# A graph layer and a mixture of experts on one core: side pieces placed two to four chunks further behind their operands

## The chip, the core and the metric

The kernel runs on one core of a Trainium2 chip. The core has a matrix engine (TensorE, "PE" in the profile, with its weight loads as "PEld"), a vector engine (VectorE, "DVE"), a scalar engine (ScalarE, "ACT"), a general engine (GpSimd, "POOL") that here mostly issues indirect DMAs, and SyncE ("SP"), whose queue issues all plain DMAs. Each engine works through its own list of instructions in order and waits on semaphores for the others. The metric is the device time of one execution in microseconds (us).

## The reference

There are N = 6250 nodes with D = 256 features, 106250 edges sorted by destination, and 8 experts with H = 1024 hidden units.

```python
# graph layer
xw  = layernorm(x) @ W
msg = xw[src] * rsqrt(max(out_deg, 1))[src][:, None]
agg = segment_sum(msg, dst)
x   = x + relu(agg * rsqrt(max(in_deg, 1))[:, None] + b)
# mixture of experts, two experts a token
xt = layernorm(x); logits = xt @ Wr + br
top_p, top_idx = top_k(softmax(logits), 2); weights = top_p / top_p.sum()
xe = layernorm(xt) * ln_g[e] + ln_b[e]          # for each expert e
y  = gelu(xe @ W1[e] + b1[e]) @ W2[e] + b2[e]
x  = x + sum over the two experts of weight * y
```

## The kernel before, in words

**Head.** The out-degrees are counted with one-hot matmuls, and a table of scaled rows `ytab` is written to device memory.

**The gather loop.** The edges are cut into 831 chunks of 128 edges; 14 chunks (`CE`) make a block, and there are 60 blocks. The loop over `CHUNKS` at the end of the kernel writes the order of the instructions out by hand: for chunk `i` it emits, in this order,

- an indirect DMA on POOL for chunk `i + LEAD` (`LEAD = 24`; `gather`, L1271), and at most one waiting scatter of routed rows (`send`, L965, into `xs`) or scatter-add of results (`add_up`, L1095, into `out`);
- the chunk's own matmuls on PE, which add its 128 rows into the block's sum `pm` by a one-hot of the destinations (L1372 up to chunk 168, after that three bf16 matmuls, L1375 to L1377, from rows of a second table `ptab`). The rows lie in a ring of 28 buffers, so the gather for chunk `c + 28` waits until PE is done with chunk `c`;
- every seven chunks the next one-hots on DVE (L223);
- side pieces, up to a budget (`run_side`, 1.2);
- pieces of the experts' work (`run_steps`), at a rate that the planner sets.

**Side pieces** are Python generators. `yield cost, wait` ends a piece and says how many chunks later the next piece may stand. They are:

- `finish(b)`, when block `b` is summed: ACT copies `pm` to `ag` (L735); a later piece turns it on PE (L741, L742) and DVE adds the result into a ring of sums (L747).
- `tile_sums(t)`, when all edges of node tile `t` are in: PE multiplies with the graph layer's weights (L781, L785), DVE computes the degree's root, the relu, and adds `x` (tile `x2`, L796), SP stores it to `out` (L807).
- `route_group(g)`, for a group of two to four tiles (`GS`): the second layernorm on DVE (L838), transposes on PE (L860), their copy on ACT (L862), logits on PE (L849), softmax and the choice of two experts on DVE and ACT, counts by matmul (L922, L923), positions on DVE, then the scatter of the rows and a list of expert steps (`batches`).

**Expert steps** (`expert_steps`). One step takes 256 rows of one expert (128 in the first eight): SP loads the rows (`xin`, L1131) and the expert's 2182 KB of weights (`w`, L1136); PE transposes (L1144), DVE scales (L1149), PE runs the first layer (L1201, into `ph`, two buffers), ACT the gelu (L1210), PE the second layer (L1220), DVE the output (L1231, L1237), POOL adds it to `out`. The planner turns a batch of steps into a rate: estimated cost of what is waiting over the chunks left until the next batch is expected (`expect`), at most 1.3 a chunk.

**Tail.** After the last chunk the remaining steps follow each other; the last batch holds ten, and more under a condition.

The tiles `x2` of the nodes' features are loaded two blocks ahead (`fetch_x`, L767) and held until the group is routed. The ring of sums is made of segments of 1024 nodes; `later` holds when the next segment's start values are loaded (`open_segment`).

Of the kernel before, what the change touches and what calls it, by code (L numbers as in the profile page):

```python
# [9 lines left out]
F32 = mybir.dt.float32  # L10
# [8 lines left out]
P = 128  # L19
# [4 lines left out]
def gnn_then_moe(  # L24
# [51 lines left out]
    NMSG = 42  # L76
    LEAD = 24
    BEHIND = 10

    TB = 256  # L80
    SB = TB // P
# [626 lines left out]
    side = []  # L708
    batches = []

    def register(engine, ap, top):
        _, (v,) = nc.values_load_multi_w_load_instructions(
            ap, engines=(engine,), min_val=0, max_val=top,
            skip_runtime_bounds_check_because="made from counts that stay in range",
            bass_reorder=False,
        )
        return v
# [13 lines left out]
    def finish(b, pm):  # L731

        s = seg(b)
        ag = s3.tile([P, D + 1], F32, tag="ag", name="ag")
        nc.scalar.copy(ag, pm)  # L735
        if b and seg(b - 1) < s:
            nc.vector.tensor_copy(ring[s][:, :, :OVER], ring[s - 1][:, :, SEGN:])
        yield 0.0, 2
        pt = psum()[:, : (KD + 1) * P].rearrange("p (k q) -> p k q", q=P)
        for k in range(KD):  # L740
            nc.tensor.transpose(pt[:, k, :], ag[:, k * P : (k + 1) * P], ident)  # L741
        nc.tensor.matmul(  # L742
            pt[:, KD, :], ag[:, D : D + 1].to_broadcast([P, P]), ident,
            start=True, stop=True,
        )
        w = register(mybir.EngineType.DVE, win_i[0:1, b : b + 1], RING - WIN)
        nc.vector.tensor_tensor(  # L747
            ring[s][:, :, bass.ds(w, WIN)], ring[s][:, :, bass.ds(w, WIN)], pt, ALU.add
        )
        for t in range(NT):  # L750
            if CLOSE[t] == b:
                side.append([now[0] + 2, 1, tile_sums(t, ring[s], t * P - SEGN * s)])
        yield 0.7, 1

    place = {}
# [6 lines left out]
    x_of = {}  # L762

    def fetch_x(t):
        v = x_of[t] = s3.tile([P, D], F32, tag="x2", name="x2", bufs=17)
        if t < NT - 1:
            nc.sync.dma_start(v, x[t * P : (t + 1) * P, :])  # L767
        else:
            nc.vector.memset(v, 0.0)
            for r0, r1 in ((0, split), (split, LASTROWS)):  # L770
                nc.sync.dma_start(v[r0:r1, :], x[t * P + r0 : t * P + r1, :])

    def tile_sums(t, sums, c0):

        g, i = place[t]
        if i == 0:
            held[g] = s3.tile([P, GMAX, 2], F32, tag="mv1", name="mv1")
        x2, mv1 = x_of[t], held[g]
        pw = psum()
        for k in range(KD):  # L780
            nc.tensor.matmul(  # L781
                pw[:, :D], sums[:, k, c0 : c0 + P], gw_sb[:, k, :],
                start=(k == 0), stop=(k == KD - 1),
            )
        nc.tensor.matmul(  # L785
            pw[:, D : D + 1], sums[0:1, KD, c0 : c0 + P], ones[0:1, 0:1],
            start=True, stop=True,
        )
        deg = s3.tile([P, 1], F32, tag="deg", name="deg")
        nc.vector.tensor_scalar(deg, pw[:, D : D + 1], 1.0, None, op0=ALU.max)  # L790
        nd = rsqrt(s3, deg, 1, "nd")
        h = s3.tile([P, D], F32, tag="h", name="h")
        nc.vector.scalar_tensor_tensor(
            h, pw[:, :D], nd, gb_sb, op0=ALU.mult, op1=ALU.add
        )
        nc.vector.scalar_tensor_tensor(  # L796
            x2, h, 0.0, x2, op0=ALU.max, op1=ALU.add
        )
        st = s3.tile([P, 6], F32, tag="bnst", name="bnst")
        nc.vector.bn_stats(st, x2)  # L800
        nc.vector.bn_aggr(mv1[:, i, :], st)
        if t < NT - 1:
            parts = ((0, P),)
        else:
            parts = ((0, split), (split, LASTROWS))
        for r0, r1 in parts:
            d = nc.sync.dma_start(out[t * P + r0 : t * P + r1, :], x2[r0:r1, :])  # L807
            for o in adds:
                tc.declare_no_dep(d.ins, o.ins, reason="rows of other tokens")
            bases.append(d)  # L810
        yield 1.1, 1
        if i == GS[g] - 1:
            side.append([now[0] + 3, 2, route_group(g, t + 1 - GS[g], mv1)])

    def running(bufs, first, n):
        a, d, i = first, 1, 0
# [7 lines left out]
    def route_group(g, t0, mv1):  # L824
# [11 lines left out]
        for q in range(n + 2):  # L836
# [15 lines left out]
                    )  # L852
                nc.vector.tensor_tensor(logits[:, i, :], pl, br_sb, ALU.add)
            if q == 0:
                yield 0.0, 2
            if 0 <= q - 1 < n:
                i = q - 1
                pt = psum()[:, : KD * P].rearrange("p (k q) -> p k q", q=P)
# [1 line left out]
                    nc.tensor.transpose(pt[:, k, :], rowt[:, i, k * P : (k + 1) * P], ident)  # L860
                turned[i] = s3.tile([P, KD, P], F32, tag="xtT", name="xtT", bufs=3)
                nc.scalar.copy(turned[i], pt)  # L862
            yield 0.9, 1
        rs2 = rsqrt(s3, mv2[:, :n, 1], n, f"l2_{n}", EPS)
        shift = s3.tile([P, GMAX], F32, tag="shift", name="shift")[:, :n]
        nc.vector.scalar_tensor_tensor(
# [31 lines left out]
        for s in range(2):  # L898
# [16 lines left out]
            if has_last:  # L915
                j = s * n + n - 1
                nc.vector.tensor_scalar(hot[:, j, :], hot[:, j, :], valid, None, op0=ALU.mult)
        yield 0.0, 4
        hotf = hot.rearrange("p j e -> p (j e)")
        w2 = 2 * n * E  # L920
        pp = psum()
# [201 lines left out]
    def expert_steps(todo, forever):  # L1123
# [133 lines left out]
    closing = {b: [t for t in range(NT) if CLOSE[t] == b] for b in range(NBE)}  # L1257

    expect = [
        end_of[CLOSE[sum(GS[: g + 1]) - 1]] + 3 * GS[g] + LEAD + 16 for g in range(len(GS))  # L1260
    ]
    def gather(i):
        b, j = CHUNKS[i]
# [81 lines left out]
    for i, (b, j) in enumerate(CHUNKS):  # L1345
# [41 lines left out]
        if i + 1 == end_of[b]:  # L1387
            side.append([i + 1, 0, finish(b, pm)])
            if b + 1 < NBE and seg(b + 1) > seg(b) and seg(b + 1) + 1 < NSEG:
                later.append((i + CE, seg(b + 1) + 1))  # L1390
        if later and later[0][0] <= i:
            open_segment(later.pop(0)[1])
        run_side(1.2)
# [101 lines left out]
```

## Time and profile before

| | |
|---|---|
| Median of 10 runs | 1903.2 us (1898.85 to 1912.02) |
| The profiled execution | 1899.83 us, of which the span of instructions is 1898.1 us |
| PE busy over the span | 1439.7 us (76%) |
| PE weight loads | 1171.0 us (62%) |
| DVE busy | 875.7 us (46%) |
| ACT busy | 395.0 us (21%) |
| POOL busy | 1153.1 us (61%) |
| Mean granted clock of TensorE | 0.877 |
| First and last chunk's matmul | 147 us and 1619 us |
| Time after the last chunk in which PE runs expert steps alone | from 1671 us on

How to read the views used below. A row of a *table by stretches* gives for each engine the busy time in that stretch, the granted TensorE clock (1.00 is full speed) and the share of time in which the DMA engines were busy. A row of *waits* says which engine sat idle before which instruction, what ended the wait, the total, how often, and the longest; `issue` and `remote` mean that the profile names nobody. A row of *groups* reads: line, engine, operation, tiles, how many | busy us, mean ns | idle time before, and what ended it. A row of a *timeline* gives start, duration, engine, line, operation, tiles, how many, and in brackets the idle time before it. Matmuls are pipelined and their ends are modelled.

### The profile page before, as it was taken

The numbers are of one execution on the slowest core, as the hardware profiler recorded it, in microseconds if no ns is written. First come the engines' busy times: TensorE is split into PE (matmuls) and PEld (weight loads), VectorE is DVE, ScalarE is ACT, GpSimd is POOL, SyncE is SP. The second block draws the span as 40 slices with busy tenths as digits, with TensorE's granted clock in tenths as the row PEclk, the third lists the DMA queues.
The fourth block names the chain that finished last, engine by engine and source line by source line (L and its number), as shares of the span: only waits on it lengthen the run. The fifth ranks groups of instructions, "written<-read, shape, count | busy, mean of one in ns | idle before, by whom it ended". The sixth has DMA issues, their size and how long they took to land. (4 is left out here: it accounts for less than half of the span.)

```text
span 1898.1 us, 23690 instructions
## 1 busy us (share of the span) xinstructions
PE 1439.7 (76%) x7890; PEld 1171.0 (62%) x7890; DVE 875.7 (46%) x3123; ACT 395.0 (21%) x978; POOL 1153.1 (61%) x1127
## 2 busy tenths in 40 slices
PE   6966454547576898767777778797789799799997
PEld 5854343446355676546556566576577587688886
DVE  8993364435253372534524435326256354732211
ACT  3662121002020121210211112112112212322221
POOL 8837767466766666667666666765766563423322
PEclk9997677778777898979789889898899799899998
DMA  7737665277575776657566676576677576576673
GB/s 223 269 115 250 192 196 186 83 275 231 175 240 182 269 230 231 192 182 232 179 217 211 197 253 193 186 240 214 198 241 231 175 232 208 152 250 189 199 218 74
DMA packets 146583, 389.50 MB, mean 205 GB/s; under 512 B 22316, under 2 KB 89364, under 8 KB 139282
## 3 DMA queue, kind: packets, MB, share of 16 engines
q0 software_dynamic: 70176, 179.11, 34.1%
q1 hardware_dynamic: 76218, 208.73, 30.4%
q8 instruction: 66, 1.08, 0.2%
q14 instruction: 67, 0.55, 0.1%
q10 hardware_dynamic: 56, 0.02, 0.0%
HBM read 324.26 MB, written 63.52 MB: 204 GB/s over the span
## 5 line engine op out<-in xcount | busy, mean ns | idle before, releaser
L1271 POOL DMA_INDIRECT msgs<-ptab,srcT x663 | 653.9, 986 | 339.3 <-issue 131.8
L1201 PE MATMUL ph<-xeT,w 128*128 128x256 f32 (+1 forms) x1792 | 457.2, 393 | 79.3 <-issue 54.7
L1220 PE MATMUL py<-w,hT 128*128 128x256 f32 x1664 | 432.8, 395 | 19.6 <-issue 16.4
L1201 PEld LDWEIGHTS ph<-xeT,w 128*128 128x128 f32 x1792 | 334.4, 208 | 127.2 <-issue 61.3
L1210 ACT ACTIVATE hT<-ph,w 128x256 f32<-128x256 f32 (+1 forms) x448 | 180.6, 456 | 853.1 <-PE ph L1201 359.8
L1220 PEld LDWEIGHTS py<-w,hT 128*128 128x128 f32 x1664 | 305.9, 198 | 55.9 <-issue 17.9
L1095 POOL DMA_INDIRECT out_x<-yo,to_all x86 | 137.9, 1604 | 179.8 <-DVE yo L1237 34.7
L1375 PE MATMUL pm<-msgs,oh 128*128 128x257 bf16 x663 | 191.3, 289 | 6.4 <-issue 6.3
L1376 PE MATMUL pm<-msgs,oh 128*128 128x256 bf16 x663 | 190.3, 287 | 6.8 <-issue 6.8
L1377 PE MATMUL pm<-msgs,oh 128*128 128x256 bf16 x663 | 190.1, 287 | 6.0 <-issue 6.0
L1149 DVE TENSOR_SCALAR xeT<-ptf,w 128x256 f32<-128x256 f32 (+1 forms) x112 | 53.5, 519 | 258.6 <-PE ptf L1144 128.6
L747 DVE TENSOR_TENSOR ring<-ring,misc 128x384 f32 x60 | 33.3, 554 | 287.0 <-remote 163.4
L1271 POOL DMA_INDIRECT msgs<-ytab,srcT x126 | 128.8, 1022 | 54.9 <-issue 33.3
L965 POOL DMA_INDIRECT xs<-rowt,pos_i x98 | 100.1, 1021 | 58.3 <-issue 44.7
L223 DVE TENSOR_TENSOR oh<-iota_w,relT 128x896 bf16<-128x896 f32 (+2 forms) x119 | 127.7, 1080 | 14.5 <-PE pm L1372 8.2
L781 PE MATMUL misc<-gw_sb,ring 128*128 128x256 f32 x196 | 70.9, 497 | 78.6 <-issue 40.5
L1372 PE MATMUL pm<-msgs,oh 128*128 128x257 f32 x336 | 103.0, 461 | 29.6 <-DVE oh L223 14.8
L1376 PEld LDWEIGHTS <-oh 128*128 128x128 bf16 x663 | 68.4, 103 | 76.2 <-issue 20.4
L1372 PEld LDWEIGHTS pm<-msgs,oh 128*128 128x128 f32 x336 | 74.4, 233 | 43.3 <-DVE oh L223 15.6
L781 PEld LDWEIGHTS misc<-gw_sb,ring 128*128 128x128 f32 x196 | 43.3, 243 | 93.5 <-issue 45.6
L381 PE MATMUL hist<-oh_hi,oh_lo 128*128 128x49 bf16 x831 | 85.4, 279 | 11.4 <-DVE oh_lo L375 10.9
L381 PEld LDWEIGHTS <-oh_lo 128*128 128x128 bf16 x831 | 82.5, 150 | 14.2 <-DVE oh_lo L375 13.8
(600 smaller groups left out, 1591.7 us busy)
## 6 DMA issues: line engine op xcount, KB each, us to landing
w<-in_wcat SPq DMA_DIRECT2D x56, 2182.0 KB
xin<-xs SPq DMA_DIRECT2D x48, 260.0 KB
msgs<-ptab,srcT POOLq DMA_INDIRECT x663
strayT<-zeros SPq DMA_DIRECT2D x1, 9216.0 KB
ptab<-part SPq DMA_DIRECT2D x24, 384.0 KB
ytab<-xres SPq DMA_DIRECT2D x7, 896.0 KB
ring<-strayT SPq DMA_DIRECT2D x4, 1536.0 KB
x<-in_x SPq DMA_DIRECT2D x48, 128.0 KB
```

Of the source, the lines that this page charges most:

```text
L223: nc.vector.tensor_tensor(oh[:, :n, :], iota_w[:, None, :].to_broadcast([P, n, WIN]), relT[:, c : c + n, None].to_broadcast([P, n, WIN]), ...
L381: nc.tensor.matmul(hist, oh_lo[:, :, c], oh_hi[:, :, c], start=(c0 + c == 0), stop=(c0 + c == NCH - 1),)
L781: nc.tensor.matmul(pw[:, :D], sums[:, k, c0 : c0 + P], gw_sb[:, k, :], start=(k == 0), stop=(k == KD - 1),)
L1095: ad = nc.gpsimd.indirect_dma_start(out=out, out_offset=bass.IndirectOffsetOnAxis(ap=to, axis=0), in_=rows, in_offset=None, compute_op=ALU ...
L1201: nc.tensor.matmul(ph[:, c - c0, :tb], w[:, k * H + c * P : k * H + (c + 1) * P], xeT[:, k, :tb], start=(k == 0), stop=(k == KD - 1),)
L1210: nc.scalar.activation(hT[:, c, :tb], ph[:, c - c0, :tb], AF.Gelu, bias=w[:, OB1 + c : OB1 + c + 1],)
L1220: nc.tensor.matmul(py[:, s, :], hT[:, c, s * P : (s + 1) * P], w[:, OW2 + c * D : OW2 + (c + 1) * D], start=(c == 0), stop=(c == HC - 1),)
L1271: nc.gpsimd.indirect_dma_start(out=to, out_offset=None, in_=table, in_offset=bass.IndirectOffsetOnAxis(ap=srcT[:, c : c + 1], axis=0),)
L1372: nc.tensor.matmul(pm, oh, msg[i % NMSG][:, : D + 1], start=first, stop=last)
L1375: nc.tensor.matmul(pm, oh, part[:, PW - D : PW + 1], start=first, stop=False)
L1376: nc.tensor.matmul(pm[:, :D], oh, part[:, D : PW - D], start=False, stop=False)
L1377: nc.tensor.matmul(pm[:, :D], oh, part[:, :D], start=False, stop=last)
```

## The change

A constant `SPARE = 4` is added, and a helper `wait(n)` that returns `n + 4` while the chunk number is below `NCK - 4 * CE` (831 - 56 = 775) and `n` after that. Six waits of the side pieces go through it:

- in `finish`, between the copy to `ag` and its transposes, 2 becomes 6; and 2 becomes 6 between the add into the ring and the tile's `tile_sums`;
- between a group's last `tile_sums` and its `route_group`, 3 becomes 7;
- in `route_group`, 2 becomes 6 after the first tile's layernorm; 1 becomes 3 between the following pieces (each with the transposes of one tile and the logits of the tile before); 4 becomes 8 between the choice of experts and the counts.

The tiles `x2` get 20 buffers for 17. `expect` moves later by `5 * SPARE + 2 * GS[g]` chunks, and the load of a ring segment by `3 * SPARE` chunks. Nothing else is changed; the same instructions are issued, in another order.

```diff
+    SPARE = 4
...
+    def wait(n):
+
+        return n + (SPARE if now[0] < NCK - 4 * CE else 0)
...
-        yield 0.0, 2
+        yield 0.0, wait(2)
         pt = psum()[:, : (KD + 1) * P].rearrange("p (k q) -> p k q", q=P)
...
-                side.append([now[0] + 2, 1, tile_sums(t, ring[s], t * P - SEGN * s)])
+                side.append([now[0] + wait(2), 1, tile_sums(t, ring[s], t * P - SEGN * s)])
...
-        v = x_of[t] = s3.tile([P, D], F32, tag="x2", name="x2", bufs=17)
+        v = x_of[t] = s3.tile([P, D], F32, tag="x2", name="x2", bufs=20)
...
-            side.append([now[0] + 3, 2, route_group(g, t + 1 - GS[g], mv1)])
+            side.append([now[0] + wait(3), 2, route_group(g, t + 1 - GS[g], mv1)])
...
             if q == 0:
-                yield 0.0, 2
+                yield 0.0, wait(2)
...
-            yield 0.9, 1
+            yield 0.9, 1 + (wait(0) >> 1)
...
-        yield 0.0, 4
+        yield 0.0, wait(4)
         hotf = hot.rearrange("p j e -> p (j e)")
...
-        end_of[CLOSE[sum(GS[: g + 1]) - 1]] + 3 * GS[g] + LEAD + 16 for g in range(len(GS))
+        end_of[CLOSE[sum(GS[: g + 1]) - 1]] + 3 * GS[g] + LEAD + 16 + 5 * SPARE + 2 * GS[g] for g in range(len(GS))
...
-                later.append((i + CE, seg(b + 1) + 1))
+                later.append((i + CE + 3 * SPARE, seg(b + 1) + 1))
```

## The prediction

> **What bounds the kernel now.** I read the page's busy times and its slices, then a table by stretches, then PE's waits, POOL's groups, and a timeline of one long wait. Page:
>
> ```profile
> PE 1439.7 (76%) x7890; PEld 1171.0 (62%) x7890; DVE 875.7 (46%) x3123; ACT 395.0 (21%) x978; POOL 1153.1 (61%) x1127
> ...
> PE   6966454547576898767777778797789799799997
> ...
> PEclk9997677778777898979789889898899799899998
> ```
>
> No engine is full over the span, but PE is full at the end and idles a fifth to half of each slice in the gather loop, where its clock is often cut. By stretches: f32 gathers; bf16 gathers; the loop's end with the last routing; expert steps alone.
>
> ```profile
> core 0: us, PE busy (x) PEld busy (x) DVE busy (x) ACT busy (x) POOL busy (x), PEclk, DMA share, GB/s
> 150.00:373.00 223.00, 118.77 (x430) 90.34 (x429) 109.99 (x373) 39.14 (x78) 144.60 (x143) 0.72 0.58 184
> 373.00:1594.00 1221.00, 940.08 (x5112) 741.89 (x5112) 533.19 (x2144) 200.38 (x479) 807.56 (x784) 0.87 0.67 215
> 1594.00:1671.00 77.00, 61.83 (x319) 51.49 (x318) 55.72 (x288) 21.02 (x46) 31.12 (x25) 0.92 0.66 188
> 1671.00:1887.00 216.00, 212.90 (x1011) 186.67 (x1009) 43.71 (x143) 50.38 (x120) 63.41 (x41) 1.00 0.64 190
> ```
>
> In the loop PE idles 223 - 119 = 104 us and 1221 - 940 = 281 us; in the tail almost nothing. PE's waits, 150 to 1600 us:
>
> ```profile
> PE misc L860 <- DVE rowt L838: 40.7, 8, 13.1
> PE misc L781 <- issue: 40.5, 13, 8.5
> PE misc L741 <- ACT ag L735: 34.0, 10, 7.2
> PE misc L781 <- DVE ring L747: 32.7, 9, 7.6
> PE misc L849 <- issue: 23.4, 6, 12.8
> PE misc L922 <- DVE hot L908: 17.8, 6, 5.8
> PE misc L849 <- ACT xtT L862: 17.6, 6, 5.4
> PE misc L741 <- issue: 17.5, 8, 4.8
> ```
>
> These are first matmuls of side pieces. With the small rows of the same lines (L781 5.4; L922 5.0 and 2.2; L741 3.9; L849 2.0 and 0.9; L860 1.9) side pieces make 245.5 us in 73 waits, 3.4 us each. The rest is mostly the experts' (L1201 <- issue 54.7) and one-hots (L1372 <- DVE oh 14.8).
>
> POOL, 373 to 1594 us:
>
> ```profile
> L1271 POOL DMA_INDIRECT msgs<-ptab,srcT x656 | 647.2, 987 | 332.5 <-issue 131.1 <-PE pm L1377 112.1 <-remote 52.9
> L965 POOL DMA_INDIRECT xs<-rowt,pos_i x79 | 81.0, 1025 | 24.8 <-issue 22.7 <-DMA xs<-rowt,pos_i 1.8 <-DMA msgs<-ptab,srcT 0.3
> L1095 POOL DMA_INDIRECT out_x<-yo,to_all x49 | 80.5, 1643 | 56.4 <-DMA out_x<-x 12.0 <-issue 9.8 <-DVE l_a L206 7.8
> ```
>
> POOL is busy 809 us, and its timeline has at least 0.30 us between two issues even back to back: 784 x 0.30 = 235. So POOL needs 1044 of 1221 us and waits 177, mostly for a buffer that PE has not given back. PE never waits for a gather (L1375 <- issue 6.3 is all that stands before a chunk's first matmul). So PE, with its waits, sets the loop's pace, and POOL stands close behind.
>
> One wait in the timeline:
>
> ```profile
> 961.35 0.39 PE L742 MATMUL misc<-ident,ag 128*128 128x128 f32 x2
> ...
> 964.01 0.42 PE L1377 MATMUL pm<-msgs,oh 128*128 128x256 bf16 x1
> ...
> 971.33 0.84 ACT L1210 ACTIVATE hT<-ph,w 128x256 f32<-128x256 f32 x2 [10.31 <-remote]
> 971.44 0.55 DVE L747 TENSOR_TENSOR ring<-ring,misc 128x384 f32 x1 [19.18 <-remote]
> ...
> 972.05 2.07 PE L781 MATMUL misc<-gw_sb,ring 128*128 128x256 f32 x4 [7.62 <-DVE ring L747]
> ```
>
> DVE was not busy: it, and ACT at the same moment, waited for PE, whose transposes are recorded as ended by 961.74 and were passed on 9.7 us later. So part of these waits is lateness of PE's own results, not of the vector engines, and distance does not cure its cause.
>
> **The change part by part.**
>
> *Six longer waits.* A chunk takes 1221 / 663 = 1.84 us, of which 940 / 663 = 1.42 is PE work. Four chunks put 5.7 us of other PE work between a piece and its operand, two chunks (L849, L860 after a group's first tile) 2.8. The mean wait of 3.4 us would go, the long ones (7 to 13 us) partly. Bounds of what ends: nothing, if the following matmuls stand still too (after 971 us: both layers need ACT's gelu, which was as late as the ring); and no more than POOL's room, 177 + (223 - 145 - 143 x 0.30) = 212 less some 18 us at the loop's end without gathers, 194 us. I take half of 245.5, 123 us, as ended, since long waits and covered ones hold about equal shares of the total. Of that I let half, 61 us, come back: `ph` has two buffers, so PE can run two pairs of L1201, four chunks at the usual rate, before it needs ACT; and POOL, which needs 1.58 us a chunk (1044 / 663), takes over wherever PE is quicker. Kept: 62 us.
>
> *Later routing.* The order of instructions in the two built programs shows a group of four spanning 59 chunks instead of 39; the first batch of expert steps comes at chunk 186 instead of 156, later ones some 32 later, the tenth at 793 for 761, the eleventh at 811 for 800, the last two (845, 857) unmoved. When the gather loop ends, 38 steps have been turned in, not 40. In the tail one step takes 14.4 us:
>
> ```profile
> 1684.51 7.19 PE L1201 MATMUL ph<-xeT,w 128*128 128x256 f32 x32
> ...
> 1698.89 1.46 PE L1201 MATMUL ph<-xeT,w 128*128 128x256 f32 x6
> ```
>
> Two steps add 28.8 us where PE is full (1.00 clock, 213 of 216 us). In the loop they free the same PE work, worth between 0 (POOL sets the pace) and 28.8; I take PE's busy share, 0.77 x 28.8 = 22. Net +7, bounds 0 and +29. What goes with them: two weight loads (2182 KB each) and row loads on SP, four scatter-adds on POOL (1.64 us each, in a stretch where POOL is busy 63 of 216 us), ACT's gelus (50 of 216): nothing.
>
> *Queues.* Between a moved piece and its old place stand chunk matmuls and experts' matmuls on PE, experts' scales and one-hots on DVE, gelus on ACT. DVE meets its ring add (L747) and degree (L790) in the same chunk as PE's piece, as before, with one-hots for the next seven chunks queued behind; PE needs those up to seven chunks later, so they stay covered. SP passes the stores (L807) with the moved pieces; weights queued behind them are as late as before. POOL's scatters (L965) move with the routing, at most one a chunk, and are as many. I cost this at nothing, bounds -10 and +10 (the 54.7 us before L1201 may shift either way).
>
> *Buffers of x, segments, expected times.* Three more tiles hold x for the longer route; without them SP would stand at a load, with weights behind it. The segment loads (1536 KB, 7 us at 215 GB/s) come 12 chunks later, with over a hundred chunks to spare. The expected times move with the batches, so rates stay, except near the end (1.22 a chunk for 1.02). All nothing.
>
> Sum against the profiled execution's 1899.8 us: -123 + 61 + 7 = -55, so 1845. The median of the runs stands 3.4 us higher: 1849.
>
> **Two rules against the rows.** PE is busy 16.8 of 50 us at a clock of 0.57 from 300 to 350 us, and 50 of 50 at 1.00 from 1700 to 1750. The Trainium skill ("TensorE: Matmul & The Clock Gate", HAM oscillation) says that idle gaps of more than about 3.4 us put PE back to half rate. By that rule, an estimate, half of the 73 waits would each save about 1.7 us more: 62 us, and 1787.
>
> Against the change: POOL and PE weight loads are each at 61 to 62%. The skill's "Perfetto Trace Analysis" (Identifying the Most-Contended Engine) has the engine of highest occupancy worked on first, and this change takes no work from any engine. By that rule nothing is gained and the two steps are lost: 1932.
>
> **The rivals.**
>
> *POOL becomes the bound and the moved steps are lost (slower).* If chunks do not come quicker, from POOL's pace or from late PE results that stall whatever stands next, the loop keeps its length and the tail grows by 28.8 us less a little: 1910 to 1932, at 1925. It decides once less than 29 us of the 245 is kept. For: POOL at 1044 of 1221; the wait at 971. Against: POOL still waits 177 us.
>
> *The waits move.* Side pieces stop waiting, L1201 and L1220 wait in their place; 20 to 35 us are kept and the steps take them: 1895 to 1910, at 1903. For: `ph`'s two buffers. Against: only 16.4 us before L1220 now.
>
> *POOL's floor.* All is kept that POOL allows, 130 to 194 us less 7 to 29: 1730 to 1790. For: the cut clock would return too. Against: the long waits.
>
> **How the numbers follow.** Forecast (1790 to 1895) 0.50, POOL's floor 0.09, waits move 0.17 (0.04 faster, 0.06 same, 0.07 slower), slower rival 0.24. So faster 0.63, same 0.06, slower 0.31; 0.2% is about what this measurement tells from no change. The range, 1785 to 1925, leaves out most of the floor case and half of the slower one: 0.2. The forecast's own range is 1790 to 1895.
>
> **What would show it.** Right: the waits before L741, L781, L860, L849, L922 fall from 245 us to about half or less; POOL's idle time shrinks by the same; the last chunk comes some 85 us earlier, with the tail after it 29 us longer; the clock in the long stretch above 0.87. Wrong: those waits go and L1201's and L1220's grow; or PE begins to wait before L1375; or the last chunk comes where it did.

## The result, and the profile after

The changed kernel takes 1933.3 us (median of 18 runs, 1919.3 to 1943.6) against 1907.0 us for the kernel before: a ratio of 1.0132, 95% interval 1.0116 to 1.0149 (here and below ratios are estimated from the single runs and can differ by up to 0.4% from the quotient of two medians). It is slower, by 1.3%; the prediction was 1849 us, and even its range ended at 1925. The profiled execution has a span of 1938.1 us (before: 1898.1).

After the change lines are numbered one higher above the helper `wait` and five higher below it, so L223 is now L224, and L741, L781, L849, L860, L922, L1201, L1220 are L746, L786, L854, L865, L927, L1206, L1225.

From the page of the changed kernel, the busy times and the slices of PE and of its clock:

```profile
PE 1450.9 (75%) x7890; PEld 1178.7 (61%) x7890; DVE 873.0 (45%) x3123; ACT 393.3 (20%) x978; POOL 1148.9 (59%) x1127
...
PE   6955547356756688688597786988888868799997
...
PEclk9997777667867889788788888989898889899998
```

The table by stretches, with the last one lengthened to the end of the expert steps (columns: stretch, its length, busy time and count of each engine, PE's clock, DMA share, GB/s):

```profile
150.00:373.00 223.00, 112.28 (x410) 87.67 (x409) 96.92 (x281) 36.53 (x72) 148.28 (x146) 0.72 0.60 189
373.00:1594.00 1221.00, 920.23 (x4949) 719.27 (x4949) 534.87 (x2204) 194.50 (x469) 792.97 (x775) 0.84 0.65 209
1594.00:1671.00 77.00, 66.78 (x349) 56.31 (x349) 51.30 (x259) 21.31 (x47) 27.74 (x20) 0.91 0.58 158
1671.00:1928.00 257.00, 246.19 (x1163) 215.60 (x1161) 57.04 (x204) 56.98 (x136) 74.15 (x50) 0.99 0.64 192
```

In the long stretch PE does less in the same 1221 us: 920 us busy for 940, at a clock of 0.84 for 0.87. The stretch of expert steps alone is 41 us longer than before. The gather loop as a whole has kept its length: the last chunk's products stand at 1626.7 us, before at 1619.3. What follows them takes 311.4 us, before 278.8. So 32.6 of the 40 us between the two profiled executions lie behind the loop and 7.4 in it.

PE's waits in the loop, 150 to 1600 us (columns: where PE waited, for what; us in total, times, longest):

```profile
PE ph L1206 <- DVE xeT L1154: 50.1, 9, 15.5
PE ph L1206 <- ACT hT L1215: 44.7, 12, 11.5
PE py L1225 <- issue: 28.1, 29, 5.6
PE misc L854 <- ACT xtT L867: 26.2, 2, 19.2
PE misc L746 <- issue: 23.4, 10, 11.3
...
PE ph L1206 <- issue: 19.1, 21, 6.9
PE misc L786 <- issue: 17.0, 7, 6.3
```

Summed by line, the side pieces wait 179.7 us where they waited 245.5. But the experts' two layers wait 153.2 us (L1206 119.6, L1225 33.6) for 93.4, and the chunks' own products 71.3 for 44.6. Altogether PE waits 410 us in this stretch; before it was 384. So 66 us ended at the side pieces and 86 came back on the instructions that now stand in their place.

POOL in the long stretch:

```profile
L1276 POOL DMA_INDIRECT msgs<-ptab,srcT x649 | 639.4, 985 | 321.5 <-issue 143.3 <-PE pm L1382 89.1 <-remote 45.4
L970 POOL DMA_INDIRECT xs<-rowt,pos_i x82 | 82.2, 1002 | 25.0 <-issue 22.8 <-DMA xs<-rowt,pos_i 1.2 <-DMA msgs<-ptab,srcT 0.6
L1100 POOL DMA_INDIRECT out_x<-yo,to_all x44 | 71.4, 1623 | 74.8 <-DVE xeT L1154 18.2 <-DVE oh L224 14.4 <-DVE l_a L207 8.7
```

Busy 793 us and 775 gaps of 0.30 us make 1026; POOL still waits some 195 us of the 1221, before it was 178. It did not come any closer to its floor.

One of the long waits of the changed kernel, in the timeline (start, duration, engine and line; in brackets the idle time before it and the releaser):

```profile
946.44 1.02 PE L854 MATMUL misc<-wr_sb,xtT 128*128 128x8 f32 x4 [8.51 <-issue]
947.32 0.67 PE L865 MATMUL misc<-ident,rowt 128*128 128x128 f32 x2
...
950.40 0.27 PE L1382 MATMUL pm<-msgs,oh 128*128 128x256 bf16 x1
...
963.07 0.94 POOL L1276 DMA_INDIRECT msgs<-ptab,srcT  x1 [2.47 <-remote]
963.58 0.84 ACT L1215 ACTIVATE hT<-ph,w 128x256 f32<-128x256 f32 x2 [17.20 <-remote]
965.05 0.17 DVE L858 TENSOR_TENSOR logits<-misc,br_sb 128x8 f32<-128x8 f32 x1 [22.38 <-remote]
965.14 0.37 ACT L867 COPY xtT<-misc 128x256 f32<-128x256 f32 x1 [0.72 <-remote]
...
965.27 2.08 PE L786 MATMUL misc<-gw_sb,ring 128*128 128x256 f32 x4 [14.60 <-DVE logits L858]
```

PE's matmuls of L854 and L865 start at 946.44 and 947.32 us and are recorded as done by 948.0 (starts are recorded, ends modelled). DVE and ACT, idle but for one gelu, get their results at 965.05 and 965.14, some 17 us later; POOL and the gelu are released within the two us before that. PE itself then waits 14.6 us at L786 for a `misc` buffer that DVE could not read out earlier. Here the operand (the ring, last written by DVE at 933.9 us) was long there; a larger distance between the piece and its operand would not have shortened this wait.

### The profile page after: what moved, and what is told of

The parts are those of the page before. It is cut to its first block, busy times and chain, and to the rows that moved or that the text cites. A ratio compares the mean times of both kernels' runs of the same rounds, so it can differ in the third digit from the quotient of the medians.

```text
span 1938.1 us, 23658 instructions
## 1 busy us (share of the span) xinstructions
PE 1450.9 (75%) x7890; PEld 1178.7 (61%) x7890; DVE 873.0 (45%) x3123; ACT 393.3 (20%) x978; POOL 1148.9 (59%) x1127
## 5 line engine op out<-in xcount | busy, mean ns | idle before, releaser
L1206 PE MATMUL ph<-xeT,w 128*128 128x256 f32 (+1 forms) x1792 | 456.9, 393 | 126.1 <-DVE xeT L1154 55.2
L1225 PE MATMUL py<-w,hT 128*128 128x256 f32 x1664 | 441.1, 399 | 33.8 <-issue 28.1
L1206 PEld LDWEIGHTS ph<-xeT,w 128*128 128x128 f32 x1792 | 334.5, 207 | 177.3 <-DVE xeT L1154 58.3
L1225 PEld LDWEIGHTS py<-w,hT 128*128 128x128 f32 x1664 | 309.6, 200 | 77.5 <-issue 36.1
L1382 PE MATMUL pm<-msgs,oh 128*128 128x256 bf16 x663 | 193.6, 292 | 13.5 <-issue 13.4
L1381 PE MATMUL pm<-msgs,oh 128*128 128x256 bf16 x663 | 194.0, 293 | 11.9 <-issue 11.8
L224 DVE TENSOR_TENSOR oh<-iota_w,relT 128x896 bf16<-128x896 f32 (+2 forms) x119 | 128.0, 1077 | 9.3 <-PE pm L1377 7.6
L1377 PE MATMUL pm<-msgs,oh 128*128 128x257 f32 x336 | 103.7, 468 | 32.4 <-issue 22.4
L1381 PEld LDWEIGHTS <-oh 128*128 128x128 bf16 x663 | 69.1, 104 | 78.7 <-issue 25.9
L1377 PEld LDWEIGHTS pm<-msgs,oh 128*128 128x128 f32 x336 | 77.2, 240 | 47.6 <-issue 23.7
L786 PE MATMUL misc<-gw_sb,ring 128*128 128x256 f32 x196 | 59.5, 432 | 52.6 <-issue 17.0
L795 DVE TENSOR_SCALAR deg<-misc 128x1 f32<-128x1 f32 x49 | 7.7, 157 | 198.3 <-PE pm L1382 68.6
L1380 PEld LDWEIGHTS <-oh 128*128 128x128 bf16 x663 | 69.7, 105 | 44.3 <-issue 21.4
```

The source lines that it names most:

```text
L224: nc.vector.tensor_tensor(oh[:, :n, :], iota_w[:, None, :].to_broadcast([P, n, WIN]), relT[:, c : c + n, None].to_broadcast([P, n, WIN]), ...
L1206: nc.tensor.matmul(ph[:, c - c0, :tb], w[:, k * H + c * P : k * H + (c + 1) * P], xeT[:, k, :tb], start=(k == 0), stop=(k == KD - 1),)
L1225: nc.tensor.matmul(py[:, s, :], hT[:, c, s * P : (s + 1) * P], w[:, OW2 + c * D : OW2 + (c + 1) * D], start=(c == 0), stop=(c == HC - 1),)
L1377: nc.tensor.matmul(pm, oh, msg[i % NMSG][:, : D + 1], start=first, stop=last)
L1380: nc.tensor.matmul(pm, oh, part[:, PW - D : PW + 1], start=first, stop=False)
L1381: nc.tensor.matmul(pm[:, :D], oh, part[:, D : PW - D], start=False, stop=False)
```

## The experiments

The runs were made on several chips, and the kernel before itself takes either some 1890 to 1910 us or some 1707 us on them. Each group of runs was made on one chip at one time, and no chip comes up twice in the groups, so the chip and the time are not told apart; "kind of chip" stands for both. The kernel before has a trace only on the longer kind. Each ratio is against the kernel before on the same chip. "The loop" is the time of the last chunk's products in the span, "the tail" what follows.

**Parts of the change, where before takes 1708.6 us.** Theory 1 was that the loop's length does not hang on the distance, and each step moved behind it costs its 14.4 us; theory 2 that the longer waits themselves cost. The expected times, segments and buffers of x alone:

```diff
-        ... + 3 * GS[g] + LEAD + 16 for g in range(len(GS))
+        ... + 3 * GS[g] + LEAD + 16 + 5 * SPARE + 2 * GS[g] for g in range(len(GS))
-                later.append((i + CE, seg(b + 1) + 1))
+                later.append((i + CE + 3 * SPARE, seg(b + 1) + 1))
-        ... name="x2", bufs=17)
+        ... name="x2", bufs=20)
```

> Only the expected times, the later segment loads and the three more buffers of x; no piece waits longer, and the batches of expert steps come when they came before. The planner then turns in 38 steps in the gather loop instead of 40, as in the changed kernel. Theory 1 (the gather loop's length is set by something that neither the distance of pieces nor two steps more or less of PE work alters, and each step moved behind the loop costs its 14.4 us): the last chunk comes within 10 us of before, and the time is 20 to 30 us above before, 1927 to 1937, that is the whole loss of the change without any longer wait. Theory 2 (the loss comes from the longer waits themselves, by waits taken over at L1201 and its like): no more than 10 us above before. My prediction's own sum would have +7.

Measured: 1734.6 us, 1.0187 (1.0141 to 1.0233); loop 1419.9, tail 312.3 us.

Only the waits of `finish` and of the sums' start, with `bufs=20`:

```diff
-        yield 0.0, 2
+        yield 0.0, wait(2)
         pt = psum()[:, : (KD + 1) * P]...
-                side.append([now[0] + 2, 1, tile_sums(...)])
+                side.append([now[0] + wait(2), 1, tile_sums(...)])
```

> Only the finish of a block and the sums of a tile stand four chunks further back (the first two of the longer waits), with the buffers of x; route_group and the expected times are as before. Batches come 8 chunks later; the gather loop turns in 40 steps as before, though one more stands in the list at its end. The waits before L741 and L781 (134 us of the 245 in before) are the ones that this edit can shorten. Theory 1: these waits shrink, others grow by the same, the last chunk stays within 10 us; time 1905 to 1922 for none to one step moved. My prediction's reasoning, kept for half of the half: 134 / 4 = 33 us saved, 1870 to 1885. Theory 2: 5 to 15 above before.

Measured: 1712.6 us, 1.0033 (1.0010 to 1.0056); loop 1425.8, tail 282.2. The waits before L741 and L781 are 16 us here, against 50 in the run before it, so the pieces do stand far enough; and it buys nothing on this chip.

Only the four waits of `route_group` (its start, the first tile, 1 + 2 chunks a tile, the counts), with the expected times and `bufs=20`:

```diff
-            side.append([now[0] + 3, 2, route_group(...)])
+            side.append([now[0] + wait(3), 2, route_group(...)])
-                yield 0.0, 2
+                yield 0.0, wait(2)
-            yield 0.9, 1
+            yield 0.9, 1 + (wait(0) >> 1)
-        yield 0.0, 4
+        yield 0.0, wait(4)
```

> Only route_group's start and pieces stand further back (four longer waits), with the expected times and the buffers of x; finish and tile sums are as before. Batches come some 22 to 24 chunks later, 38 steps are turned in by the loop's end. The waits before L849, L860 and L922 (111 us) can shrink. Theory 1: last chunk within 10 us of before, time 1927 to 1945 (two steps, or three since five stand in the list). My prediction's reasoning: 111 / 4 = 28 saved against 29 to 43 lost, 1907 to 1922. Theory 2: as theory 1, but with the waits before L1201 grown by more than in the run with the front alone.

Measured: 1749.4 us, 1.0246 (1.0201 to 1.0291); loop 1436.4, tail 311.5.

No longer wait at all, but the batches held back, with the expected times and `bufs=20`:

```diff
         if not last_group:
-            yield 0.0, 4
+            yield 0.0, 34 if now[0] < NCK - 4 * CE else 4
         batches.append((g, code, row_i, wrow_i))
```

> The kernel before with the batches of expert steps held back by 30 chunks behind their routing, and the expected times and x buffers of the change; no piece of routing stands further from its operand. 38 steps are turned in by the loop's end. Theory 1: last chunk within 10 us of before, and 1927 to 1945, as with the whole change. Theory 2: at most 10 above before. If the later batches rather than the distance make the waits at L1201 grow, the waits there show it here too: near 112 us as after the change, against 71 before.

Measured: 1738.3 us, 1.0187 (1.0148 to 1.0226); loop 1429.0, tail 307.7. PE waits 24 us before L1201 here, against 35 us in the run of the expected times alone; so on this kind of chip later batches do not make that wait grow.

What follows: all runs with 38 steps turned in have a tail of 308 to 312 us, the one with 40 has 282. On this kind of chip the moved steps alone make nearly all of the loss, with or without longer waits; with the longer waits of `route_group` the loop is also 7 to 16 us longer than in the other two runs with 38 steps, which is not explained. These loops, however, are 190 us shorter than those of the first traces. The long stretch of the kernel with the two front waits, from the table by stretches:

```profile
373.00:1400.00 1027.00, 840.98 (x5022) 690.90 (x5022) 516.19 (x2089) 198.16 (x474) 777.01 (x755) 0.91 0.75 246
```

POOL's waits of the same kernel in this stretch:

```profile
POOL msgs L1276 <- issue: 99.8, 326, 0.6
POOL msgs L1276 <- PE pm L1382: 49.6, 140, 3.0
```

Busy 777 and 755 x 0.30 make 1004 of 1027 us: POOL is at 98% and simply sets the pace. Its waits for PE are 0.35 us each, little more than the gap between two issues, and none has the releaser "remote".

**The two kernels again, and two mixtures, where before takes 1889.3 us.** The kernel before, for its trace:

> The kernel before, unchanged, for a trace on the chip that the experiments run on, which took 1709 us where the first measurement took 1907. If that chip differs in the late results of PE, their episodes (updates over 2 us behind the recorded end, 504 us of the first trace's loop) are short here, below 120 us, and the gather loop ends some 190 us earlier; if it differs in something else (DMA, the clock of the tail), the difference is spread over the whole span, the tail too.

Measured: 1880.7 us in its one run; this chip is like that of the first traces. Loop 1599.0, tail 279.9 us. PE's late results are there in the same measure.

The changed kernel:

> The changed kernel, unchanged, where late results of PE are rare. Theory 1 (what the loop takes does not hang on the distance, each step moved behind the loop costs 14.4 us): two steps and a part of a third, 1.5 to 2.5% above before, 26 to 43 us, as in the run with the later batches alone (1.0187) and the one with the routing's waits (1.0246). My prediction's theory, with late results out of the way: the waits are the vector engines' own, distance ends them, and the change is at least level, 0.985 to 1.00.

Measured: 1909.7 us, 1.0109 (1.0070 to 1.0147); loop 1589.4, tail 309.7. The loop is 10 us shorter with two steps less in it, the tail 30 longer. Side pieces wait 146.7 us for 257.5, L1201, L1220 and the chunks 229.2 for 113.8, all together 388 for 374: again everything came back. The expectation was written for the other kind of chip; its second theory is not tested by this run.

All waits, segments and buffers of the change with the expected times left as before:

```diff
     expect = [
-        ... + 3 * GS[g] + LEAD + 16 + 5 * SPARE + 2 * GS[g] for g in range(len(GS))
+        ... + 3 * GS[g] + LEAD + 16 for g in range(len(GS))
```

> All six longer waits, the later segments and the buffers, with the expected times left as before. Batches come as late as in the change and 38 steps are turned in, as there, but the rates are higher towards the end of each batch. If the moved steps make the loss: within 0.5% of the changed kernel, 1.015 to 1.025. If the laxer expected times make it: within 0.3% of before.

Measured: 1931.6 us, 1.0203 (1.0142 to 1.0264); loop 1625.3, tail 308.0. The tail is that of the change; the loop is 36 us longer than with the laxer times.

The opposite edit on the kernel before:

```diff
-        ... + 3 * GS[g] + LEAD + 16 for g in range(len(GS))
+        ... + 3 * GS[g] + LEAD + 16 - 30 for g in range(len(GS))
-            pace["rate"] = min(1.3, ...)
+            pace["rate"] = min(2.0, ...)
```

> The opposite edit, on the kernel before: expected times 30 chunks earlier and the cap on the rate at 2.0, no other change. 43 steps are turned in by the loop's end instead of 40 and 33 are done instead of 31. Theory 1, each step costs 14.4 us behind the loop and next to nothing in it: 2 to 3 steps, 29 to 43 us faster, 0.975 to 0.983. If PE has no room left in the loop (PE's pace sets it): within 0.4% of before, since the loop grows by what the tail loses.

Measured: 1985.5 us, 1.0523 (1.0474 to 1.0572): a clear miss. The tail did fall, from 279.9 to 244.9 us, as expected; the loop grew from 1599 to 1734. The slices of PE and POOL from the page of this kernel:

```profile
PE   6955473576763895774858929849759589979997
...
POOL 8836757565656557465576664675665646144332
```

PE now comes in bursts. Counted in the trace by chunks of the bf16 part, 221 of 662 lie in runs of four or more with no matmul of the experts beside them: they hold 62 of the 76 row scatters and take 325 us, of which POOL needs 309 (busy time and 0.30 us an issue). The other 441 chunks take 1004 us, 2.28 us each, where POOL needs only 720. A batch of steps is done in some 42 of the 70 chunks between two batches, at up to 2.0 units of expert work a chunk, and nothing is left for the 28 chunks in which POOL scatters the next group's rows. In the kernel before, on the same chip, there is no such run; its 662 chunks take 1198 us, POOL needing 1023. POOL's and PE's long stretches now stand one after the other instead of side by side. The run of the waits with the old expected times has a milder form of it: 219 chunks without expert work take 325 us, the other 443 take 916; the changed kernel on that chip has 36 such chunks, and its loop is 36 us shorter.

**What sets the loop: PE or POOL? Where before takes 1705.8 us.** Row scatters spread out:

```diff
-            for waiting in (rows_out, sums_out):
+            for waiting in ((rows_out, sums_out)[i % 2],):
-                (now[0] + BEHIND, partial(send, s, i)) ...
+                (now[0] + BEHIND - 4, partial(send, s, i)) ...
         if not last_group:
-            yield 0.0, 4
+            yield 0.0, 1
         batches.append(...)
```

> The kernel before with POOL's row scatters (L965) taken only at even chunks and the scatter-adds (L1095) only at odd ones, instead of one of either at every chunk; the scatters fall due four chunks earlier and the batches wait three chunks less, so that batches come when they came (155, 281, 355, ... for 156, 282, 355), and 40 steps are turned in as before. A group's scatters then take 16 chunks instead of 8. Theory 1, late results of PE are bound to the density of row scatters: the episodes shrink by a third or more and the loop by 30 to 100 us, 0.945 to 0.985, on a chip where before takes some 1890 to 1907; on a chip where it takes 1709, within 0.5%. Theory 2, POOL's pace (2.6 us a chunk with a scatter, 1.3 without) sets the loop only inside the clusters while PE idles there: the same sign, half as much, 15 to 40 us. Theory 3, neither: within 0.4%.

Measured: 1709.2 us, 1.0017 (0.9996 to 1.0037); loop 1432.3, tail 274.8.

One product of three left out:

```diff
-            nc.tensor.matmul(pm[:, :D], oh, part[:, D : PW - D], start=False, stop=False)
```

> The kernel before without the middle one of the three bf16 products of a chunk (L1376), so the middle part of each message is missing from the sums. PE has 190 us less to do in the loop (663 x 0.287). If PE's own work sets the loop between the clusters of scatters: 80 to 170 us faster, 0.91 to 0.96, where before takes some 1890; if POOL sets it: within 1% where before takes 1709, and at most 30 us where before takes 1890. If late results stall whatever stands next, work removed goes into the stalls only in part: 30 to 80 us, 0.96 to 0.985.

Measured: 1706.2 us, 1.0004 (0.9980 to 1.0027); loop 1427.6, tail 287.5. The time does not move. The 190 us of the expectation, however, is the sum of the product's own durations. The three products of a chunk overlap: in the first trace they start at 954.78, 954.89 and 955.00 us and last 0.27 us each. What PE really has less to do is shown by its busy time, in the run with the spread scatters on the same chip and in this one:

```profile
373.00:1400.00 1027.00, 849.92 (x5001) 691.80 (x5001) 520.96 (x2092) 196.64 (x468) 776.38 (x756) 0.91 0.76 245
373.00:1400.00 1027.00, 801.82 (x4356) 642.80 (x4354) 517.05 (x2082) 195.94 (x468) 780.06 (x755) 0.89 0.76 245
```

That is 48 us less, at a somewhat lower clock.

The loop's scatter-adds left out:

```diff
-                    waiting.pop(0)[1]()
+                    one = waiting.pop(0)[1]
+                    if waiting is rows_out:
+                        one()
```

> The kernel before without the scatter-adds of the loop (L1095, 49 in the long stretch), so the sums of those steps are missing from the output. POOL has 49 x 1.94 = 95 us less to do in the loop. If POOL sets the loop: 80 to 100 us faster (0.94 to 0.955). If PE and its late results set it, POOL only blocks PE inside the clusters: 0 to 40 us, 0.98 to 1.00.

Measured: 1625.3 us, 0.9527 (0.9485 to 0.9569), 80 us less, as much as POOL's pace gives: 8 adds stand in the loop for 54, and 46 are 89 us at 1.94 each. Loop 1348.1, tail 278.3.

The expected times, segments and buffers alone, once more:

> The same kernel as the run of the expected times and later segments alone (it was 1.0187 on a chip where before took 1709): two steps move behind the loop, no piece waits longer. On the same chip: 1.015 to 1.023 again. On a chip where before takes some 1890 and PE's work and late results set the loop, the loop gives part of the two steps back: the tail grows by 29, the loop falls by 10 to 25, 1.002 to 1.011. If it is 1.015 or more there too, the two steps are not worth anything in the loop on either chip.

Measured: 1731.2 us, 1.0151 (1.0102 to 1.0199); loop 1421.0, tail 309.9.

What follows: on this kind of chip POOL sets the loop alone; in the traces of this kind its busy time and gaps make 98 to 99% of the time from 150 us to the last gather. What PE waits for in the loop costs nothing here, and taking waits away gains nothing.

**The same question where before takes 1909.3 us.** All full steps put by and added behind the loop:

```diff
-            if sb == SB and deferring[0] and done[0] % 3 == 0:
+            if sb == SB and deferring[0]:
-        if beat % 16 == 8:
+        if beat % 5 == 2:
             add_back()
```

> The kernel before with every full step of the loop put by and added behind the loop, instead of every third (one pair of rows taken back every 5 beats instead of every 16): some 40 of the loop's 49 scatter-adds (L1095, 1.94 us of POOL each with its gap) go to the tail, where POOL is busy 63 of 216 us. Where POOL sets the loop (before at 1706 to 1709): 60 to 80 us faster, 0.953 to 0.965. Where before takes some 1890 and PE's work and late results set it: 0 to 40 us faster, 0.98 to 1.00. If the tail's end then hangs on the adds: up to 20 us less of that in either case.

Measured: 1961.2 us, 1.0273 (1.0227 to 1.0319), slower. The loop ends at 1570.7 us, but the tail takes 391.8: 14 adds stand in the loop for 54, and 90 in the tail for 50. Put against a loop of about 1628 for the kernel before on this chip (1909.3, less 1.7 outside the span, less a tail of 280), the loop gave back 57 of POOL's 78 us. POOL did not become quicker by all of it because it waits longer for PE's buffers (160 us at L1271 after L1377 in the long stretch, 107 and 112 in the two traces of the kernel before). The tail could not carry the adds. DVE waited 189 us there, ten times, to write into `yo` (L1237), whose three buffers hang on the adds behind the ones taken back:

```profile
DVE yo L1237 <- DMA out_x<-yo,to_all: 189.0, 10, 35.2
```

Two products of three left out:

```diff
-            nc.tensor.matmul(pm, oh, part[:, PW - D : PW + 1], start=first, stop=False)
-            nc.tensor.matmul(pm[:, :D], oh, part[:, D : PW - D], start=False, stop=False)
-            nc.tensor.matmul(pm[:, :D], oh, part[:, :D], start=False, stop=last)
+            nc.tensor.matmul(pm, oh, part[:, PW - D : PW + 1], start=first, stop=last)
```

> The kernel before with one of a chunk's three bf16 products left (L1375), so the two lower parts of each message are missing from the sums. PE has 380 us less to do in the loop. Where POOL sets the loop: within 0.5% of before, as without one product (1.0004). Where before takes some 1890: if PE's own work sets the loop between the clusters, it falls to near POOL's floor, 130 to 190 us, 0.90 to 0.93; if late results stall whatever stands next and it is their length that counts, 60 to 130 us, 0.93 to 0.97; if POOL sets the loop there too, within 1%.

Measured: 1891.4 us, 0.9913 (0.9885 to 0.9940); loop 1611.8, tail 281.1. The 380 us of the expectation are again a sum of overlapping durations; PE's busy time in the long stretch falls by 113 us, from 940 in the first trace to 828, at a clock of 0.82 for 0.87. That is worth about 18 us. The stretch, from the table by stretches:

```profile
373.00:1594.00 1221.00, 827.55 (x3853) 643.39 (x3852) 537.28 (x2172) 200.83 (x483) 811.18 (x787) 0.82 0.67 216
```

POOL's waits of that kernel in the same stretch:

```profile
POOL msgs L1271 <- issue: 128.7, 413, 1.3
POOL msgs L1271 <- PE pm L1375: 90.4, 118, 3.9
POOL msgs L1271 <- remote: 64.4, 43, 4.0
```

And one of ACT's:

```profile
ACT hT L1210 <- remote: 195.2, 23, 22.2
```

POOL needs 811 + 787 x 0.30 = 1047 of 1221 us and waits 174, as in the kernel before (1044 and 177). PE, with less to do, still returns buffers late, and ACT still waits up to 22 us for results that PE was recorded to have made long before. So less load on PE does not shorten these waits.

The changed kernel with the deferred adds of the first run of this group:

> The changed kernel with the same edit as the run with all full steps put by. Against that run it shows the change where POOL has 78 us less to do. If distance is worth something once POOL is out of the way: the difference to that run is below the change's own (20 to 26 us), or negative. If only the two steps behind the loop count: 25 to 35 us above that run.

Measured: 1958.6 us, 1.0299 (1.0240 to 1.0359), within the uncertainty of the run without the change. Its loop is 24 us shorter (1546.5), its tail 15 longer (407.2). With POOL relieved the change does shorten the loop, but two steps less stand in it too, and the tail's end hangs on the adds here, so the two are not separated.

**Once more on the scatters, where before takes 1706.1 us.** The spread scatters, same edit as above:

> Again the kernel before with row scatters at even chunks and scatter-adds at odd ones, same batches, same 40 steps (1.0017 on a chip where before takes 1706). Where before takes some 1900: if late results of PE hang on the density of row scatters, the loop loses 30 to 100 us, 0.945 to 0.985; if they hang on the number of scatters, or on something else, within 0.7%. Where it takes some 1706, as before: within 0.4%.

Measured: 1707.7 us, 1.0013 (0.9988 to 1.0038); loop 1430.4, tail 275.7.

The two front waits, same edit as above:

> Again the two longer waits before L741 and L781 alone, 40 steps turned in (1.0033 where before takes 1709). Where before takes some 1900 and the waits before those lines are 134 us: by my prediction's reasoning, kept for half of the half, 0.983 or less. If what the loop takes is set by POOL and the length of the late results, and not by where PE's own pieces stand: 1.000 to 1.008, the loop unchanged within 10 us and the tail longer by no more than one step.

Measured: 1711.7 us, 1.0044 (1.0025 to 1.0064); loop 1431.5, tail 283.4.

Each row scatter made twice:

```diff
+    xs_b = dram.tile([NXS, XW], F32, name="xs_b")
...
             scatters.append(sc)
+            if not last_group:
+                sc = nc.gpsimd.indirect_dma_start(out=xs_b, ... in_=rowt[:, i, :], in_offset=None)
```

> The kernel before with each row scatter of the loop made twice, the second copy into a second table that nobody reads: some 92 more on POOL, 1.33 us each with the gap, 122 us, and as many 520 KB writes. Where before takes 1706 and POOL sets the loop: 1.06 to 1.075. Where it takes some 1900: if late results follow the row scatters, the loop grows by those 122 us and by a doubling of the 200 us or so of lateness inside the clusters, 1.09 to 1.18; if they do not, by at most the 122 us, 1.03 to 1.065.

Measured: 1818.0 us, 1.0675 (1.0632 to 1.0719): 112 us more, a little less than POOL's own time for them (loop 1528.2, tail 288.6). The second copies write 133 KB each by the queue's bytes, not the 520 KB of the expectation. No wait of POOL, ACT or DVE has the releaser "remote" in this trace. Twice the scatters do not make PE's results late on this kind of chip. That the three runs fell on such a chip leaves the question open that they were meant for: whether fewer or thinner scatters would make PE's results less late on the other kind. Nor were the expected times alone, or the front waits alone, run there; that the two steps make the loss on that kind rests on its tails: 245 us with 43 steps turned in, 279 to 281 with 40, 308 to 311 with 38.

None of the runs that do the whole computation is faster than the kernel before on its chip, so there is no better version to show.

## Why the prediction was wrong

*What bounds the kernel.* "PE, with its waits, sets the loop's pace, and POOL stands close behind" had it the wrong way round. Leaving out two products, 113 us of PE's busy time in the long stretch, took 0.9% (18 us) where before takes 1909 us; leaving out one, 48 us, took nothing where it takes 1706. Putting off 78 us of POOL's work shortened the loop by about 57 us on the former, and leaving out adds (89 us) took 80 us on the latter. On the shorter kind of chip POOL's queue sets the loop alone. On the longer kind, where the change was predicted, the loop is POOL's 1044 us in the long stretch plus some 175 us in which POOL waits, mostly for buffers that PE returns late; that these two add up is read from the traces and from two runs, and what makes PE late is open.

*Six longer waits.* Of the 123 us forecast to end at the lines named, 66 ended in the first pair of traces and 111 in the second. The step that failed is the next one, "Of that I let half, 61 us, come back". It had to let all of it: the waits at L1201, L1220 and the chunks grew by 87 us in the first pair and 115 in the second. So the 62 us put down as kept measured nothing, and the loop ended 7 us later in the first pair and 10 us earlier, with two steps less in it, in the second. The prediction held the reason in hand, with its lower bound of "nothing, if the following matmuls stand still too" and the wait at 971 us, and gave it half the weight. In the lines of the changed kernel at 965 us the gelu and a gather are released late together with the side pieces; what moves in front of such a stop only waits there instead.

*Later routing.* The tail's term was right: 28.8 us forecast, 32.6 and 29.8 measured in the two pairs of traces, 22 to 35 on one chip between runs with 38 and with 40 steps turned in; and with 43 steps, on the longer kind, the tail is 35 us shorter than with 40. The 22 us that the two steps were to free in the loop were mostly not there: by the run with two products left out (18 us for 113) two steps' 28.8 us are worth some 5, an estimate, and the run of the expected times alone lost 25 us with a tail some 30 longer. "Net +7" should have been near +24. With 0 for the waits and +24 for the steps the sum gives 1931 on the 1907.0 that the kernel before took beside the changed one; measured 1933. (1845 and 3.4 make 1848, not 1849, which changes nothing.)

*Queues, buffers, segments.* Costed at nothing and rightly, as far as the runs tell: the front waits alone, with the buffers, cost 0.3 to 0.4%, within the 10 us given. "The expected times move with the batches, so rates stay" was too quick: where the times stay and the batches move, the loop is 36 us longer, and 30 chunks earlier with a higher cap cost 5.2%.

*The clock.* The estimate by the rule on idle gaps ("TensorE: Matmul & The Clock Gate") was that fewer long waits return 62 us. No run here shows such a gain: the side waits fell from 73 to 47, other waits took their place, and the clock of the long stretch went from 0.87 to 0.84.

*The most contended engine.* The rule in "Perfetto Trace Analysis" (Identifying the Most-Contended Engine) judges PE not by its matmul time but by the operations done and by its weight loads; by these loads PE (62%) and POOL (61%) stood level, and it did not tell which of them sets the loop. The outcome that the prediction drew from it, nothing gained and the steps lost, is what happened. POOL's share hides that it is the bound on the shorter kind of chip: its 0.30 us between two issues are not counted as busy, and make 235 us here.

*The rivals.* The slower one came true, and a little past its end at 1932: the loop kept its length and the tail grew. It was named for POOL "or late PE results that stall whatever stands next", and both hold. "Against: POOL still waits 177 us" was the wrong argument: those waits hardly moved (195 us after the change, 174 with two products left out), so they were no room that a quicker PE could use. That the waits would move to L1201 and L1220 was also right, but the 20 to 35 us said to be kept were not.

## What to carry to other kernels

Waiting time before an engine's instructions is only worth what it takes from the queue that sets the pace; add the gaps between issues to a DMA-issuing engine's busy time before deciding which queue that is. If several engines are released in the same moment, by a result that was recorded as made long before, the wait belongs to that result, and moving instructions about only changes who stands in it. And count what a longer pipeline pushes past the end of the loop that covers it: here two steps of 14.4 us are about the whole loss. And when several instructions overlap on an engine, take what leaving them out saves from its busy time, not from the sum of their durations: 113 us here, not 380.

## What the chip did that was not expected

The same program differs by some 11% between chips: the kernel before takes 1889 to 1909 us on some and 1706 to 1709 us on others. The first chunk stands at 146 to 147 us and the tail, with 40 steps turned in, takes 279 to 281 us on the longer kind and 275 to 289 on the shorter; the difference lies in the gather loop, which ends at 1599 to 1619 us against some 1430. The kernel's granted clock is 0.87 to 0.88 on the longer kind and 0.90 to 0.92 on the shorter; which follows from which is not shown. On the shorter kind the releaser "remote" does not appear among the waits of POOL, ACT and DVE in the eleven traces' loops. On the longer kind it does, as in the changed kernel's first trace, in ACT's waits, 373 to 1594 us:

```profile
ACT hT L1215 <- remote: 165.7, 15, 30.5
ACT xtT L867 <- remote: 45.7, 6, 10.7
ACT ag L740 <- remote: 39.2, 3, 28.5
ACT slot L931 <- remote: 32.4, 4, 10.7
```

These are the late results. Pairing, in the loop, the gelus, the ring adds, the copies to `xtT` and the reads of logits and degrees with the last matmul that each needs, in the order of the program, 103 of them start over 2 us after both that matmul's recorded end and the last work of their own engine in the first trace of the kernel before, 109 after the change and 109 with two products left out; these waits cover 423, 504 and 516 us of the loop. On the chip with both kernels they cover 430 and 422 us. In seven traces of the shorter kind it is 6 to 16 waits, 13 to 59 us. In the first trace 126 of the 423 us lie in the clusters of row scatters (each up to 8 us behind its last one), which take 304 of the loop's 1470 us, so the scatters are at most a part of the story. What makes the late results, and why some chips have them, was not found: doubling the scatters on a chip of the shorter kind brought none of the releasers "remote", and thinner scatters were only run on chips of that kind.
